# Order of VectorE's routing chain in four routed FFNs, and products of constants in TensorE's waits

## The chip, the cores and the metric

One core of a Trainium2 chip runs the whole program once per launch. The metric is the device time in microseconds of that launch. TensorE (PE) multiplies matrices, VectorE (DVE), ScalarE (ACT) and GpSimd (POOL) work on vectors, and SyncE (SP) issues transfers, as ACT and POOL can do too.

## The reference

The kernel computes four layers of a "macaron" network on x of shape (2, 512, 256) in float32, 1024 tokens in all. Each layer is half an FFN, an attention or state-space block, and half an FFN again, each on a normalised input, without learned scale, and each added to x:

```
x = x + 0.5 * ffn(layernorm(x));  x = x + attn(layernorm(x));  x = x + 0.5 * ffn(layernorm(x))
```

- Layer 0: a routed FFN with 32 experts of width 176, six chosen per token by softmax, with a capacity of slots for each expert, and a shared expert of width 352; then a retention block.
- Layer 1: a linear map with binarised weights, and sparse attention.
- Layer 2: an FFN that mixes 8 experts, and a Mamba2 block with 8 heads.
- Layer 3: a routed FFN with 8 experts of width 176, two chosen by sigmoid, and a shared expert of width 176; then a Mamba2 block with 64 heads.

So there are four routed FFNs, two in layer 0 and two in layer 3. Each is

```
scores = softmax or sigmoid of x @ router;  top k of each token
pos    = running count of an expert's tokens: the slot of each (token, expert)
y      = sum over the chosen experts of weight * (silu(x @ wg) * (x @ wu)) @ wd
out    = y + (silu(x @ sg) * (x @ su)) @ sd          # the shared expert
```

## The kernel before

x stays on chip. The 1024 tokens are NC = 8 chunks of 128, four (CB) in each of two batches or halves. A product over 256 channels is two passes (KD = 2). Every matmul in float32 shows as two records in the trace, and a weight load (PEld) goes with each.

A routed FFN runs in these steps. The line numbers are those of the profile of the kernel before.

1. For each batch: `layernorm` makes xn (VectorE, and POOL for the root, L217 and L218), TensorE transposes it (ps_tr, L177) and xT is evicted. `logits` (L317) follows: for each of the 8 chunks two matmuls with xT as the weights and the router as the moving operand, 32 columns or 8. Transposes and logits stand in a written order on TensorE and ACT (`in_order`).
2. VectorE: the scores (L730 to L735, or L748 on ACT), `topk` (L299 to L309) which ends in the mask, and then `slot_lists`. That makes sl_pre (running counts over chunks, L425) and sl_row (a number for each chosen slot, L434 and L435); TensorE makes ps_pos from sl_pre and the mask (L427, L428); VectorE makes slot numbers from it and two one-hot tables, sl_ol and sl_oh (L454 and L456 for 32 experts, L459 and L465 for 8); TensorE multiplies these (ps_sl, L473) and turns the result (ps_slt, L493). This gives sl_get and sl_put, the row numbers for the gathers and for the rows written back. In between the mask is put on the scores (L670 to L675) and the result is sent to a table in memory.
3. `shared_unit`, once for each half, on TensorE behind the logits: for each block of the shared width (three for layer 0: 128, 128, 96; two of 88 for layer 3) pg and pu (L365), silu on ACT (L368), h = s * scale * pu on VectorE (L369), and then acc (L375), one block behind; at the end x gets acc added (L393).
4. `experts_sparse`: POOL gathers the tokens of a tile (L527), `turn_x` transposes them (ps_xe, L541), ps_gu, he, ps_he, ps_ye follow (L551 to L576), and POOL scatters the rows (L581). [...]
5. A branch holds the tiles beyond the usual number; it is not taken here. The next stage loads the rows and adds them to x (L705 to L718).

Where no order is written by hand, a scheduler picks the order of each engine's instructions from its own estimate of when their inputs are ready. `issue_after` and `in_order` are the two means to say it by hand: the first keeps what is issued inside it behind one named instruction, the second chains the instructions of the named engines in the order written.

The stages that the change touches outside of the FFNs: layer 1's start (ps_add, L711, adds the FFN's rows on TensorE), and the start of the two Mamba blocks. There the input is transposed (ps_tr, L177 in layer 2, L272 by chunks in layer 3), then come pd (the step sizes, L1620), pp (the projections, L1679, each followed by a convolution on VectorE and ACT), ps_row and ps_cum (running decays, L1646 and L1664), pb and pm (L1709, L1710), and pt (transposes of the convolved input, L1761).

Of the kernel before, what the change touches and what calls it, by code (L numbers as in the profile page):

```python
# [10 lines left out]
F32 = mybir.dt.float32  # L11
AF = mybir.ActivationFunctionType
ALU = mybir.AluOpType
# [5 lines left out]
P = 128  # L19
B, S, D = 2, 512, 256  # L20
T = B * S
NC = T // P
CB = S // P
# [60 lines left out]
class Net:  # L84
# [69 lines left out]
    def rsqrt(self, out, in_, scale=1.0):  # L154

        self.nc.scalar.activation(out, in_, AF.Sqrt, bias=self.eps, scale=scale)
        self.nc.vector.reciprocal(out, out)

    def settle(self, b, n=CB, psum=None):


        parts = self.pending.get(b, [])
        while len(parts) > CB - n:
            parts.pop(0)(psum)
        if not parts:
            self.pending.pop(b, None)
# [66 lines left out]
    def layernorm_T(self, es, psum):  # L233


        xT = es.enter_context(self.tc.tile_pool(name="xT", bufs=1)).tile([P, KD, T], F32, name="xT")
        p = es.enter_context(self.tc.tile_pool(name="ln", bufs=1))

        made = {}

        def measure(b):
            made[b] = self.scales(p, b)

        def norm(b):
            made[b] = self.layernorm(p, p.tile([P, CB, D], F32, tag="xn", name="xn"), b, *made[b])

        def turn(b, k):
            self.transpose_tokens(made[b], xT, psum, b, k)

        def row(b):  # L250
            if b in self.pending:
                by_chunks(b)
                return
            measure(b)
            norm(b)
            for k in range(KD):
                turn(b, k)

        def by_chunks(b):

            xn = p.tile([P, CB, D], F32, tag="xn", name="xn")
            ps = [psum.tile([P, S], F32, tag="mm", name="ps_tr") for _ in range(KD)]
            ms = {}
            for cc in range(CB + 1):
                if cc < CB:
                    self.settle(b, cc + 1)
                    ms[cc] = self.scale(p, b * CB + cc, b * CB + cc)
                if cc > 0:
                    j = cc - 1
                    self.centre(xn[:, j, :], b * CB + j, *ms[j])  # L270
                    for k in range(KD):
                        self.nc.tensor.transpose(  # L272
                            ps[k][:, j * P : (j + 1) * P], xn[:, j, k * P : (k + 1) * P], self.ident
                        )
            for k in range(KD):
                self.evac(xT[:, k, b * S : (b + 1) * S], ps[k])

        return xT, row, measure, norm, turn
# [30 lines left out]
        nc.vector.tensor_tensor(gt, gt, eq, ALU.add)  # L309
        return gt  # L310

    def logits(self, pool, psum, xT, wT, e):
        lg = pool.tile([P, NC, e], F32, name="lg")
        ps = psum.tile([P, NC, e], F32, tag="mm", name="ps_lg")
        for c in range(NC):
            for k in range(KD):
                self.nc.tensor.matmul(  # L317
                    ps[:, c, :], xT[:, k, c * P : (c + 1) * P], wT[:, k, :], start=(k == 0), stop=(k == KD - 1)
                )
        self.nc.vector.tensor_copy(lg, ps)  # L320
        return lg

# [28 lines left out]
        at = [(i * bw, min((i + 1) * bw, f)) for i in range(n)]  # L351
        return [(gv[:, :, a:b], uv[:, :, a:b], dv[: b - a, i, :], b - a) for i, (a, b) in enumerate(at)]

    def shared_unit(self, work, psA, psM, xT, blocks, half, scale):

        nc = self.nc
        cols = slice(half * S, (half + 1) * S)
# [2 lines left out]
        def front(gv, uv, bw):  # L360
            pg = psM.tile([P, S], F32, tag="mm", name="pg")
            pu = psM.tile([P, S], F32, tag="mm", name="pu")
            for ps, wv in ((pg, gv), (pu, uv)):
                for k in range(KD):
                    nc.tensor.matmul(ps[:bw], wv[:, k, :], xT[:, k, cols], start=(k == 0), stop=(k == KD - 1))  # L365
            s = work.tile([P, S], F32, tag="s", name="s")
            h = work.tile([P, S], F32, tag="h", name="h")
            nc.scalar.activation(s[:bw], pg[:bw], AF.Silu)  # L368
            nc.vector.scalar_tensor_tensor(h[:bw], s[:bw], scale, pu[:bw], ALU.mult, ALU.mult)  # L369
            return h  # L370

        def back(h, dv, bw, first, last):
# [37 lines left out]

    def slot_lists(self, sb, tp, psM, mask, e, n, cap, r):


        nc = self.nc
# [1 line left out]
        HI = n // LO  # L418
        ET = CT // HI
        NG = e // (ET * P // CT)  # L420

        pre = tp.tile([P, NC + 1, e], F32, name="sl_pre")
        nc.vector.memset(pre[:, 0, :], 0.0)
        for c in range(NC):
            nc.vector.tensor_tensor(pre[:, c + 1, :], pre[:, c, :], mask[:, c, :], ALU.add)  # L425
        pos = psM.tile([P, NC + 1, e], F32, tag="mm", name="ps_pos")
        nc.tensor.matmul(pos, self.ones, pre, start=True, stop=False, skip_group_check=True)  # L427
        nc.tensor.matmul(pos[:, :NC, :], self.c["lt"], mask, start=False, stop=True, skip_group_check=True)  # L428

        first = tp.tile([P, NC], F32, name="sl_first")  # L430
        nc.vector.tensor_scalar(first, self.c["icol"], float(r), float(r - 1), ALU.mult, ALU.add)
        row = tp.tile([P, NC, e], F32, name="sl_row")
        for c in range(NC):
            nc.vector.tensor_tensor_scan(row[:, c, :], self.ones[:, :e], mask[:, c, :], 0.0, ALU.mult, ALU.add)  # L434
        nc.vector.tensor_tensor(row, row, first.unsqueeze(2).to_broadcast([P, NC, e]), ALU.add)  # L435
        full = sb.tile([P, 1], F32, name="sl_full")
        nc.vector.tensor_reduce(full, pos[:, NC, :], AX.X, ALU.max)
        keep = tp.tile([P, NC, e], F32, name="sl_keep")
# [67 lines left out]
    def experts_sparse(self, ew, ps, xes, table, rows, lists, w, ex, f, tiles, per, ahead=4, wp=None):  # L506
# [28 lines left out]
            return xe  # L535

        def turn_x(n, xe, nt):
            pt = ps.tile([P, KD, nt * P], F32, name="ps_xe")
            for k in range(KD):
                for i in range(nt):  # L540
                    nc.tensor.transpose(pt[:, k, i * P : (i + 1) * P], xe[:, i, k:D:KD], self.ident)  # L541
            xeT = ew.tile([P, KD, nt * P], F32, name=f"xeT{n % 2}")
            self.evac(xeT, pt)
            return xeT
# [25 lines left out]
        def down_(n, e, js, hT, wd):  # L570
            nt = len(js)
            y = ew.tile([P, nt, D], F32, name=f"ye{n % 4}")
            py = ps.tile([P, nt, D], F32, name=f"ps_ye{n % 2}")
            for i in range(nt):
                for q in range(2):
                    nc.tensor.matmul(  # L576
# [47 lines left out]
    def moe(self, pre, names, E, F, K, FS, PER, tiles, cap, r, scores, scale):  # L624
# [6 lines left out]
        with ExitStack() as es:  # L631
# [7 lines left out]
            with ExitStack() as fs:  # L639
# [6 lines left out]
                with tc.tile_pool(name="ln", bufs=1) as lp:  # L646
                    tv = table[:, :D].rearrange("(b c p) d -> b p c d", p=P, b=B)
                    rT = self.router_weights(sb, psM, router, E)
                    tail, xns = {}, []
                    with self.in_order(tail, ("PE", "Activation")):  # L650
                        for b in range(B):
                            xn = lp.tile([P, CB, D], F32, name=f"xn{b}")
                            self.layernorm(lp, xn, b, *self.scales(lp, b))
                            xns.append(xn)
                            for k in range(KD):
                                self.transpose_tokens(xn, xT, psM, b, k)
                        s = self.logits(sb, psM, xT, rT, E)
                        for b in range(B):
                            nc.scalar.dma_start(tv[b], xns[b])
                if cap < T:  # L660
# [3 lines left out]
                    for c in range(NC):  # L664
                        nc.gpsimd.dma_start(rv[c, :, :K, :], zero.unsqueeze(1).to_broadcast([P, K, D]))
                m = sb.tile([P, NC], F32, name="m")
                scores(s, m)
                mask = self.topk(sb, s, E, K)
                get, put, full = self.slot_lists(lists, sb, psL, mask, E, PER * P, cap, r)
                nc.vector.tensor_tensor(s, s, mask, ALU.mult)  # L670
                nc.vector.tensor_reduce(m, s, AX.X, ALU.add)
                nc.vector.tensor_scalar(m, m, 1e-20, None, ALU.add)
# [4 lines left out]
                blocks = self.load_shared(sg, su, sd, FS)  # L677
                with tc.issue_after(tail["PE"]):
                    for half in range(B):
                        self.shared_unit(work, psA, psM, xT, blocks, half, 0.5)  # L680
                over = lists.tile([1, 1], I32, name="over")
                nc.vector.tensor_scalar(over, full[0:1, :], float(len(tiles) * P), None, ALU.is_gt)
            ew = es.enter_context(tc.tile_pool(name="f0e", bufs=1))
# [420 lines left out]
    def l1(self):  # L1104
# [19 lines left out]
        with ExitStack() as es:  # L1124
# [173 lines left out]


            with tc.tile_pool(name="a1m", bufs=4, space=PSUM) as psM:  # L1300
                for c in range(NC + 4):
                    if c < NC:
                        front(c)
# [262 lines left out]
    def mamba(self, pre, win, wout, nh):  # L1566
# [14 lines left out]
        with ExitStack() as es:  # L1581
# [27 lines left out]
            def decay_sums(b):  # L1609
# [29 lines left out]
                nc.vector.tensor_scalar(t1, d, 1e-18, None, ALU.max)  # L1639
                nc.scalar.activation(jb[:, bs, :], t1, AF.Ln)  # L1640
                yield

                cr = wk.tile([nh, 2, S], F32, tag="cr", name="cr", bufs=1)
                ps = psM.tile([nh, S], F32, tag="mm", name="ps_row")
# [56 lines left out]
                return conv(wb[:, :, P : 2 * P], NX + 1, b, CT[:, b * S : (b + 1) * S])  # L1701

            def products(b):
                pb = psM.tile([P, CB, P], F32, tag="mm", name="pb")
                pm = psM.tile([P, CB, P], F32, tag="mm", name="pm")
                for cc in range(CB):
# [49 lines left out]
                return taps, rest  # L1756

            def prep_back(u, m):
                pt = psM.tile([P, CB, P], F32, tag="mm", name="pt")
                for cc in range(CB):  # L1760
                    nc.tensor.transpose(pt[:, cc, :], u["xc"][:, m, cc * P : (cc + 1) * P], self.ident)  # L1761
                nc.scalar.copy(u["xt"][:, :, m * P : (m + 1) * P], pt)  # L1762

                n = u["g"] * NM + m
                nc.scalar.mul(u["xc"][:, m, :], u["xc"][:, m, :], dcol[:, n : n + 1])
# [178 lines left out]
            later = {}  # L1944
            tail = {}
            with self.in_order(tail, ("PE", "Activation", "DVE")):
                row(0)
                fetch_wx(*order[0])
                d0, d1 = decay_sums(0), decay_sums(1)
# [180 lines left out]
```

## Time and profile before

| What | Value |
|---|---|
| Time, median of 3 runs | 2017.6 us (2016.25 to 2018.17) |
| The profiled execution's own time | 2018.74 us |
| Its span, first to last instruction | 2016.9 us |
| Mean granted clock of TensorE | 0.923 |
| First routed FFN, start to last ps_ye | 0 to about 244 us |
| Second routed FFN | about 440 to 672 us |
| Third and fourth | about 1156 to 1265, and 1879 to 1996 us |
| Mamba block of layer 2, of layer 3 | from 945 us, and from 1278 to 1876 us |

How to read the lines of the profile: in a timeline a row has the start, the length from the first to the last of the group, the engine, the line, the operation, out<-in, tile and moving size, and xN for the number of records. In brackets stands how long the engine had been idle before it, and what released it. "PE 1748.0 (87%)" is busy time and its share of the span. PEclk gives the granted clock of TensorE in 40 equal slices, in tenths of full speed. In a table of windows a row has the window, its length, and for each engine its busy time and number of instructions, then the granted clock, the DMA share and GB/s.

### The profile page before, as it was taken

How to read it: one execution, taken by the hardware profiler on the slowest of the kernel's cores; microseconds unless marked ns; L12 is line 12 of the kernel's file. 1: busy time of each engine (PE TensorE's matmuls, PEld its weight loads, DVE VectorE, ACT ScalarE, POOL GpSimd, SP SyncE). 2: the span in 40 equal slices, each digit the busy share in tenths (PEclk: the TensorE clock that was granted, in tenths of full speed). 3: DMA queues.
4: the chain of work that ended last, by engine and by line, in shares of the span. 5: the costliest groups of instructions: out<-in, count | busy, mean ns of one | idle time of the engine just before them, and what ended most of it. 6: DMA issues, size and time to landing. Idle time of an engine off the chain costs nothing. (4 is left out here: it accounts for less than half of the span.)

```text
span 2016.9 us, 29547 instructions
## 1 busy us (share of the span) xinstructions
PE 1748.0 (87%) x10566; PEld 1243.7 (62%) x10566; DVE 1145.4 (57%) x2673; ACT 796.8 (40%) x1340; POOL 903.6 (45%) x889
## 2 busy tenths in 40 slices
PE   6899769788999678789788989589999899999885
PEld 4677636465777545454465457357777677777564
DVE  4433276226333376556584643478777787777533
ACT  1123224311233134301661012268777677777111
POOL 3477655310777430100140026136657456767253
PEclk9899989888999889979897989699999999999788
DMA  8266440050556600000230013434454444543133
GB/s 312 82 189 190 147 178 12 11 167 13 170 185 185 214 27 1 2 21 1 95 106 22 3 54 98 137 123 149 152 168 147 147 147 159 172 149 118 44 97 96
DMA packets 117439, 226.47 MB, mean 112 GB/s; under 512 B 22382, under 2 KB 68828, under 8 KB 117014
## 3 DMA queue, kind: packets, MB, share of 16 engines
q1 hardware_dynamic: 88134, 170.17, 25.8%
q0 software_dynamic: 20608, 48.45, 7.5%
q10 hardware_dynamic: 8528, 5.72, 0.9%
q8 instruction: 92, 1.51, 0.3%
q14 instruction: 77, 0.63, 0.1%
HBM read 195.59 MB, written 41.81 MB: 118 GB/s over the span
## 5 line engine op out<-in xcount | busy, mean ns | idle before, releaser
L527 POOL DMA_INDIRECT xe<-table,sl_get x176 | 180.3, 1024 | 211.1 <-DVE sl_get L503 122.0
L551 PE MATMUL ps_gu<-we,xeT 128*128 128x352 f32 x704 | 234.2, 476 | 3.1 <-DVE xeT L130 3.1
L581 POOL DMA_INDIRECT rows<-ye,sl_put x176 | 176.8, 1005 | 82.7 <-issue 41.4
L1686 DVE SCALAR_TENSOR_TENSOR xc<-pp,L_attn_cols,xc 128x511 f32<-128x511 f32 (+2 forms) x216 | 161.4, 747 | 28.7 <-ACT xc L1682 23.4
L576 PE MATMUL ps_ye<-we,hT 88*128 88x256 f32 x704 | 168.1, 379 | 2.9 <-ACT ye L132 1.7
L556 DVE SCALAR_TENSOR_TENSOR he<-se,xe,ps_gu 128x176 f32<-128x176 f32 x176 | 69.9, 397 | 176.1 <-ACT se L555 167.0
L551 PEld LDWEIGHTS ps_gu<-we,xeT 128*128 128x128 f32 x704 | 130.8, 197 | 62.1 <-issue 6.0
L576 PEld LDWEIGHTS ps_ye<-we,hT 88*128 88x128 f32 x704 | 133.4, 190 | 36.5 <-ACT ye L132 3.6
L1813 PE MATMUL pz<-xT,wt 128*128 128x128 f32 x1152 | 143.3, 278 | 12.4 <-ACT xt L1762 6.2
L1789 DVE SCALAR_TENSOR_TENSOR lm<-lm,jb,top 128x128 f32<-128x128 f32 x576 | 153.6, 341 | 0.0
L1679 PE MATMUL pp<-xT,wx 128*128 128x512 f32 x288 | 143.2, 621 | 4.8 <-issue 1.6
L1813 PEld LDWEIGHTS pz<-xT,wt 128*128 128x128 f32 x1152 | 135.9, 193 | 17.8 <-issue 9.3
L555 ACT ACTIVATE se<-ps_gu 128x176 f32<-128x176 f32 x176 | 55.8, 317 | 228.2 <-PE ps_gu L551 228.2
L1898 PE MATMUL yacc<-wt,y 128*128 128x256 f32 x576 | 143.0, 391 | 0.9 <-POOL y L1868 0.6
L1868 POOL TENSOR_TENSOR y<-y,sg 128x512 f32<-128x512 f32 x72 | 91.8, 1274 | 106.3 <-DVE y L1867 104.8
L1806 POOL TENSOR_TENSOR ce<-ce,CT 128x1024 f32<-128x1024 f32 x54 | 127.9, 2369 | 0.0
L1898 PEld LDWEIGHTS yacc<-wt,y 128*128 128x128 f32 x576 | 104.0, 190 | 23.7 <-issue 10.1
L1518 PE MATMUL ps_y<-w8T,xT 128*128 128x512 f32 x256 | 118.4, 617 | 0.0
L1841 PE MATMUL py<-lm,xt 128*64 128x128 f32 x1152 | 108.2, 282 | 10.6 <-DVE lm L1798 3.9
L1798 DVE TENSOR_TENSOR lm<-lm,M 128x1024 f32<-128x1024 f32 x72 | 87.2, 1215 | 46.7 <-ACT lm L1794 44.1
L1879 POOL TENSOR_TENSOR sqs<-sqs,sq 128x512 f32<-128x512 f32 x56 | 71.3, 1274 | 89.0 <-ACT sq L1878 89.0
L217 POOL TENSOR_SCALAR ln_rstd<-ln_mv 128x4 f32<-128x4 f32 x15 | 3.5, 235 | 234.9 <-DVE ln_mv L209 223.7
(402 smaller groups left out, 3465.3 us busy)
## 6 DMA issues: line engine op xcount, KB each, us to landing
lm<-rows SPq DMA_DIRECT2D x72, 512.0 KB
ce<-rows SPq DMA_DIRECT2D x54, 512.0 KB
rows<-zero POOLq DMA_DIRECT2D x16, 768.0 KB, 9.4
y<-rows SPq DMA_DIRECT2D x16, 768.0 KB
we<-in_L_ffn_w_gate_dram SPq DMA_DIRECT2D x64, 176.0 KB
we<-in_L_ffn_w_up_dram SPq DMA_DIRECT2D x64, 176.0 KB
we<-in_L_ffn_w_down_dram SPq DMA_DIRECT2D x64, 176.0 KB
we<-in_L_ffn_w_dram SPq DMA_DIRECT2D x48, 176.0 KB
```

Source lines behind the costliest of these rows:

```text
L527: nc.gpsimd.indirect_dma_start(xe[:, i, :], None, table, bass.IndirectOffsetOnAxis(get[:, e * per + j : e * per + j + 1], 0), bounds_check ...
L551: nc.tensor.matmul(pg, xeT[:, k, i * P : (i + 1) * P], wgu[:, :, k], start=(k == 0), stop=(k == KD - 1))
L576: nc.tensor.matmul(py[:, i, :], hT[:, q, i * P : (i + 1) * P], wd[:, q, :], start=(q == 0), stop=(q == 1))
L581: put_rows = nc.gpsimd.indirect_dma_start(rows, bass.IndirectOffsetOnAxis(put[:, e * per + j : e * per + j + 1], 0), y[:, i, :], None, bou ...
L1518: nc.tensor.matmul(ps, xT[:, k, cs], self.w8T[:, k, 2 * e2 : 2 * e2 + 2, :], start=(k == 0), stop=(k == KD - 1))
L1679: nc.tensor.matmul(pp, wv[:, k, :], xT[:, k, b * S : (b + 1) * S], start=(k == 0), stop=(k == KD - 1))
L1686: nc.vector.scalar_tensor_tensor(out[:, 3 - w :], pp[:, : S - 3 + w], cw[:, m, w : w + 1], out[:, 3 - w :], ALU.mult, ALU.add)
L1789: nc.vector.scalar_tensor_tensor(k["lm"][:, h, :], k["lm"][:, h, :], jb[:, k["c"], n : n + 1], top, ALU.add, ALU.min)
L1806: nc.gpsimd.tensor_tensor(k["ce"], k["ce"], ct, ALU.mult)
L1813: nc.tensor.matmul(pz[:, m, :], u["wz"][:, kk, m * P : (m + 1) * P], xT[:, kk, c * P : (c + 1) * P], start=(kk == 0), stop=(kk == KD - 1),)
L1841: nc.tensor.matmul(py[i * HP : (i + 1) * HP, m, :], w[:, h * HP : (h + 1) * HP], v[:, h, :], start=(m == 0 and n == 0), stop=(n == len(src ...
L1898: nc.tensor.matmul(yacc[cc // 2][:, cc % 2, :], k["y"][:, m, :], u["wo"][:, m, :], start=(u["g"] == 0 and m == 0 and cc % 2 == 0), stop=(u ...
```

## The change

There are two kinds of edit.

VectorE's order. In each routed FFN the scores, the top k and the counts (sl_pre, sl_row and sl_first, now in `slot_counts`) are chained on VectorE. The multiplications h of the first half of the shared expert are kept behind the last of them; those of the second half are free as before.

Products of constants. A helper, `warm`, issues n matmuls identity times a 128x256 constant into a PSUM tile that nobody reads. They are put: four ahead of each batch's transposes in a routed FFN, one between the logits of each two chunks (7), two ahead and two behind the first `turn_x` of the experts, 18 at the start of layer 1, and in the Mamba blocks at the start (4 in layer 2, 18 in layer 3), between the chunks' transposes in layer 3 (3), ahead of ps_row (4), of pb (4), and of one pt (3). The branch that isn't taken gets some too; 141 are executed.

```diff
+    def warm(self, psum, n, tag="mm", w=256):
+        ps = psum.tile([P, S], F32, tag=tag, name="warm")
+        for _ in range(n):
+            self.nc.tensor.matmul(ps[:, :w], self.ident, self.c["le"][:, :w], start=True, stop=True)
...
                     self.centre(xn[:, j, :], b * CB + j, *ms[j])
+                    if j < CB - 1:
+                        self.warm(psum, 1)
...
-    def logits(self, pool, psum, xT, wT, e):
+    def logits(self, pool, psum, xT, wT, e, warm=False):
...
+            if warm and c < NC - 1:
+                self.warm(psum, 1)
...
-            nc.vector.scalar_tensor_tensor(h[:bw], s[:bw], scale, pu[:bw], ALU.mult, ALU.mult)
+            with self.tc.issue_after(behind) if behind else nullcontext():
+                nc.vector.scalar_tensor_tensor(h[:bw], s[:bw], scale, pu[:bw], ALU.mult, ALU.mult)
...
+    def slot_counts(self, tp, mask, e, r):
+        nc = self.nc
+        first = tp.tile([P, NC], F32, name="sl_first")
+        nc.vector.tensor_scalar(first, self.c["icol"], float(r), float(r - 1), ALU.mult, ALU.add)
+        pre = tp.tile([P, NC + 1, e], F32, name="sl_pre")
+        nc.vector.memset(pre[:, 0, :], 0.0)
+        for c in range(NC):
+            nc.vector.tensor_tensor(pre[:, c + 1, :], pre[:, c, :], mask[:, c, :], ALU.add)
+        row = tp.tile([P, NC, e], F32, name="sl_row")
+        for c in range(NC):
+            nc.vector.tensor_tensor_scan(row[:, c, :], self.ones[:, :e], mask[:, c, :], 0.0, ALU.mult, ALU.add)
+        nc.vector.tensor_tensor(row, row, first.unsqueeze(2).to_broadcast([P, NC, e]), ALU.add)
+        return pre, row
...
         def turn_x(n, xe, nt):
+            if n == 0:
+                self.warm(ps, 2, tag="ps_ye1")
...
+            if n == 0:
+                self.warm(ps, 2, tag="ps_ye1")
...
                         for b in range(B):
+                            self.warm(psM, 4)
                             xn = lp.tile([P, CB, D], F32, name=f"xn{b}")
...
-                        s = self.logits(sb, psM, xT, rT, E)
+                        s = self.logits(sb, psM, xT, rT, E, warm=True)
...
-                scores(s, m)
-                mask = self.topk(sb, s, E, K)
-                get, put, full = self.slot_lists(lists, sb, psL, mask, E, PER * P, cap, r)
+                with self.in_order(tail, ("DVE",)):
+                    scores(s, m)
+                    mask = self.topk(sb, s, E, K)
+                    counts = self.slot_counts(sb, mask, E, r)
+                get, put, full = self.slot_lists(lists, sb, psL, mask, *counts, E, PER * P, cap, r)
...
-                        self.shared_unit(work, psA, psM, xT, blocks, half, 0.5)
+                        self.shared_unit(work, psA, psM, xT, blocks, half, 0.5, None if half else tail["DVE"])
...
             with tc.tile_pool(name="a1m", bufs=4, space=PSUM) as psM:
+                self.warm(psM, 18)
...
+                if b == 0:
+                    self.warm(psM, 4)
                 cr = wk.tile([nh, 2, S], F32, tag="cr", name="cr", bufs=1)
...
             def products(b):
+                if b == 0:
+                    self.warm(psM, 4)
...
             def prep_back(u, m):
+                if u["b"] == u["g"] == 0 and m == 2:
+                    self.warm(psM, 3)
...
             with self.in_order(tail, ("PE", "Activation", "DVE")):
+                self.warm(psM, 4 if few else 18)
```

In the instruction streams the counts of POOL, SP, ACT and VectorE are the same before and after, and TensorE has the products of constants in addition. What moves besides: on TensorE the first acc goes behind the pg and pu of all three blocks and behind ps_pos in layer 0, and in layer 3 ps_pos goes ahead of the acc of the first half; on VectorE the three or two h of the first half go behind sl_row, the steps on the scores (L670 to L675) go ahead of the sl_row scans, the first half's two additions of acc go behind sl_oh (in layer 3 behind its first step), and sl_get goes one place ahead in the last three FFNs. On ACT the transfer of the scores' table goes one place ahead in the two FFNs of layer 0.

## The prediction

> **What bounds the kernel now.** I read section 1 and the slices of the page first, then the timelines of TensorE and VectorE in the four routed FFNs and at the starts of the attention stages, then windows of the granted clock.
>
> ```profile
> PE 1748.0 (87%) x10566; PEld 1243.7 (62%) x10566; DVE 1145.4 (57%) x2673; ACT 796.8 (40%) x1340; POOL 903.6 (45%) x889
> PEclk9899989888999889979897989699999999999788
> ```
>
> TensorE is busy 87% of 2016.9 us, at a granted clock of 0.923 on average. The windows show 1.00 or 0.50, so (1 - 0.923) x 2 x 2016.9 = 310 us ran at half clock. The slices below 9 are the seams between stages. In the expert loops TensorE is busy 20.00 of 20.00 us at clock 1.00, so what a seam saves is carried to the end. The second routed FFN (from 440 us) shows such a seam; first TensorE, then VectorE:
>
> ```profile
> 449.92 6.88 PE L317 MATMUL ps_lg<-routerT,xT 128*128 128x32 f32 x32
> 456.61 3.76 PE L365 MATMUL pg<-xT,wsh 128*128 128x512 f32 x4
> 460.16 2.96 PE L365 MATMUL pu<-xT,wsh 128*128 128x512 f32 x4
> 462.95 1.88 PE L365 MATMUL pg<-xT,wsh 128*128 128x512 f32 x4
> ...
> 472.84 0.65 PE L427 MATMUL ps_pos<-sl_pre,cst 128*128 128x288 f32 x2
> ...
> 507.81 5.06 PE L551 MATMUL ps_gu<-we,xeT 128*128 128x352 f32 x8 [0.78 <-DVE xeT L130]
> ```
> ```profile
> 463.23 0.69 DVE L369 SCALAR_TENSOR_TENSOR h<-s,pu 128x512 f32<-128x512 f32 x1 [2.58 <-PE pu L365]
> 466.66 0.69 DVE L369 SCALAR_TENSOR_TENSOR h<-s,pu 128x512 f32<-128x512 f32 x1 [0.73 <-PE pu L365]
> ...
> 475.26 0.69 DVE L393 TENSOR_TENSOR x<-x,acc 128x512 f32<-128x512 f32 x1
> ...
> 477.32 6.56 DVE L454 TENSOR_SCALAR sl_ol<-sl_hl 128x256 f32<-128x256 f32 x32
> 483.79 7.09 DVE L456 SCALAR_TENSOR_TENSOR sl_oh<-sl_hl,sl_row 128x256 f32<-128x256 f32 x16
> ```
>
> The same four matmuls of pg take 3.76 us cold and 1.88 warm; the first ps_gu takes 5.06 against 2.53 later. ps_sl (490.93) waits for sl_oh, so VectorE's chain from the logits to sl_oh sets when the gathers and the experts start. Inside it stand h, which wait for a pu that the cold clock delays, and two adds of acc that nothing urgent needs. The fourth FFN shows the same (h waits 2.47 and 2.61 us), the third less (1.27 and 2.62). In the first FFN VectorE is busy without a break from 34.64 to 61.9.
>
> How the clock moves is seen at the third FFN (columns: window, length, busy time of PE, PEld, DVE, ACT and POOL, clock, DMA):
>
> ```profile
> 1158.63:1162.05 3.42, 3.42 (x19) 3.42 (x17) 1.38 (x2) 1.17 (x2) 1.75 (x4) 0.50 0.02 5
> 1162.05:1165.46 3.41, 3.41 (x29) 3.20 (x30) 0.23 (x1) 0.00 (x0) 0.00 (x0) 1.00 0.90 306
> 1165.46:1168.88 3.42, 3.42 (x5) 1.08 (x4) 1.74 (x20) 3.31 (x4) 0.00 (x0) 0.50 0.01 4
> ```
>
> It changes at steps of 3.41 us. A stretch of transposes brought it up; the next, full of logits matmuls (8 columns on a 128x128 weight load), brought it down again though PE is marked busy throughout. So logits alone do not hold it, and long products do.
>
> **The change, part by part.** A warm product is 128x256 in float32, two records as ps_ye has them (its 4 records advance by 0.86 us): 0.43 us at full clock, 0.86 at half. 141 are executed, 76 in the FFNs (19 in each) and 65 in three attention stages: 61 us at full clock. What counts is how much of that stands in front of work that was ready.
>
> First FFN. VectorE is gated by ACT's exponential at 34.19, so warm products before the logits cost nothing and bring nothing; the cover is that wait (6.03 us), and without it they would cost 3 us. The two adds of acc (1.37 us) leave the chain, waits for ps_pos come back: -0.5. In front of the experts the clock is low from 76.61 to 83.44; two warm products before ps_xe (hidden in the wait for xe) and two behind it (0.86 us against the 0.78 that xeT takes) should keep it up: ps_gu 5.06 -> about 3: -2.0.
>
> Second FFN. Four warm products before each batch's transposes lie in waits of 2.29 and 2.44 us (1.72 needed). Second transposes 2.30 -> about 1.0. Logits: 32 records near 0.093 us (the warm rate that the third FFN shows) are 3.0 us, with 7 warm products 6.0 instead of 6.88. Their end moves from 456.83 to 455.2. At 1.72 us for each of pg and pu the third pu ends at 465.5; VectorE without its waits (2.58, 0.73, 0.35) has its counts by about 465, so ps_pos, now behind the third pu, runs at 465.6 to 466.7. Then 2.1 us of the old steps and three h (2.0 us), which are now here: sl_ol at 471.0 instead of 477.32, -6.3. TensorE's next duty is acc (24 records, 5.2 us) and the second half (six by 1.72): done near 483.5, before sl_oh at 484.7. That cover is only about 1 us: if it fails, TensorE is the next bound and the gain shrinks by that much. First ps_gu: -2.1. Sum -8.4.
>
> Third FFN. Both xn were ready and TensorE worked without a break, so eight warm products and the seven in the logits are delay: logits end 1165.1 -> 1171.1, +6.0. Against it pg and pu are warm (3.30 and 2.26 -> 1.72 each) and the waits of 1.27 and 2.62 go; ps_pos, behind four of them, moves from 1176.67 to 1178.0; with the adds of acc out and an h in, sl_ol is 0.6 later. sl_get goes ahead of the adds (POOL was released at 1194.71 by the add, 0.8 after sl_get): -0.5. ps_gu, after an idle of 5.06 us that four products do not fill, may still start cold: -0.8, between 0 and -2.5. Sum -0.7.
>
> Fourth FFN. Here both batches of transposes wait (2.02 and 2.43), logits end 1896.33 -> 1894.5, ps_pos 1907.67 -> 1901.5, two adds out, one h in: sl_ol 1910.81 -> 1904.0, -6.8; ps_gu -0.8. Sum -7.6.
>
> Attention starts:
>
> ```profile
> 686.16 5.22 PE L711 MATMUL ps_add<-y,cst 128*128 128x256 f32 x12 [12.91 <-DMA y<-rows]
> 1278.08 0.66 PE L272 MATMUL ps_tr<-cst,xn 128*128 128x128 f32 x2 [13.24 <-DVE xn L198]
> 1283.90 3.68 PE L1620 MATMUL pd<-wb,xT 128*128 128x64 f32 x16 [0.57 <-DVE xT L130]
> 1287.37 5.84 PE L1679 MATMUL pp<-xT,wb 128*128 128x512 f32 x8
> ```
>
> L3's Mamba: the other engines resume at 1268.59, so 18 warm products run from there, first at half clock, and end near 1277.7, inside the wait for xn; three more lie between the chunks. pd 3.68 -> 1.9 and pp 5.84 -> 3.44 would be -4.2; the later warm groups stand in waits of 2.72 and 2.51 us and save pp at 1301.84 (3.74) 1.9 more, but VectorE is busy 8.87 of 10 us there and keeps most of it. I take -4.5, between -8 and +1. L1's start: the same 18 from about 680.1 end near 689.8, so the first ps_add, released at 686.16, starts 3.6 us late but runs 2.6 instead of 5.22: +1; the DMA share there is 0.96 to 1.03 and y comes no earlier, so 0, between -2 and +4. L2's Mamba: four warm products stand before transposes that waited only 1.19 us: +1.7; the cold pp (3.78, 2.69, 3.38 instead of 1.88) give about -3: -1.5, between -4 and +3.
>
> SP, POOL and ACT issue the same instructions in the same order (ACT's table DMA moves one place ahead, between two silu with idle time around); no queue is moved past another.
>
> [...]
>
> Sum: -2.5 - 8.4 - 0.7 - 7.6 - 4.5 + 0 - 1.5 = -25.2. The profiled execution took 2018.74 (span 2016.9 and 1.84 around it), 1.1 above the median of 2017.6: 1993.5 from the one, 1992.4 from the other; I say 1993.
>
> **Rivals.** (1) The order pays, the warm products only pay for themselves: ps_pos then comes behind cold pg and pu (end of the third pu 469.8, sl_ol -2.0; L3's two -3.6 each; -0.5): with sl_get -10 to -11, 2007. For it: four logits stretches of 3 us added work, and window phases that differ between executions. Against it: the halved durations. (2) The warm products hold the clock nearly everywhere, TensorE's second half in the FFNs included, and Mamba's conv chains follow: -38, 1980. (3) Slower: warm products stand in TensorE's queue ahead of ready work and the clock does not rise[...]. Then a logits stretch costs 6.88 + 7 x 0.86 = 12.9 us, the third FFN +15, the groups of 18 take 15.5 us each and end at 695.6 and 1284.1, behind work that was ready at 686.16 and 1278.08 (+9 and +6, with 2.6 more between L3's chunks), L2 +3.4: +36 in all, while the second and fourth FFN lose their gain: 2053 at full price. It decides from about half of the places on (half of +36, half of -25: +5, 2023). For it: a window full of logits records did bring the clock down. Against it: 256 columns are eight times the logits' 32, and ps_ye of that size runs at 1.00. (4) Nothing to tell: the order's gain meets the delays within 0.2% (4 us, which is about what a measurement of this kernel can tell from no change).
>
> **Numbers.** Forecast 0.53 (1986 to 2001), rival 1 0.23, rival 2 0.12, rival 3 0.08, rival 4 0.04. The range 1978 to 2011 takes in the first two and most of the third. Faster 0.88, same 0.04, slower 0.08.
>
> **Signs.** In the profile after: no wait of h for pu ahead of sl_pre; ps_pos near 465.6 and 1901.5 (each stage's own shift allowed); sl_ol about 6 us earlier in FFNs two and four, unchanged in three; logits with warm products near 6.0 us; pd near 1.9 in L3; mean clock near 0.95 or above. I am wrong if the clock stays near 0.923 (then rival 1 or 3), or if ps_sl waits for the second half's pu instead of sl_oh.

## The result, and the profile after

The changed kernel took 2001.72 us (median of four, 1999.13 to 2004.27) against 2017.64: a ratio of 0.9922, 95% interval 0.9905 to 0.9939. It is 15.9 us faster, where 24.6 were forecast. A second set of runs gave the same ratio, 0.9922 (0.9903 to 0.9940).

The page of the profiled execution (1999.13 us, so the quickest of the four) has busy time by engine and the granted clock in 40 slices:

```profile
PE 1774.9 (89%) x10848; PEld 1271.5 (64%) x10848; DVE 1148.2 (57%) x2673; ACT 797.3 (40%) x1340; POOL 904.5 (45%) x889
PEclk8999979899999988979897999899999999999998
```

The mean clock is 0.950 instead of 0.923, so (1 - 0.950) x 2 x 1997.3 = 200 us ran at half clock instead of some 310. In both profiles the granted clock is recorded as 1.00 or 0.50 and nothing else; it changes 67 times before and 55 times after, and within 0.01 us all changes of a profile lie on one grid of 3.41 us. (Ahead of the first change, at 62.96 and 18.82 us, 1.00 is recorded, but in the kernel before the first pg, at 27.05, took 3.76 us, and after it the first products, at 12.10, took 3.61 where the same eight records took 1.89 later: these stretches are missing from the half-clock time.) TensorE has 282 records and 282 weight loads more, two of each for each of the 141 products, and is busy 27 us longer, in a span 20 us shorter. The second FFN's seam, in the timelines of TensorE and of VectorE:

```profile
459.19 1.96 PE L376 MATMUL pg<-xT,wsh 128*128 128x512 f32 x4
460.99 1.88 PE L376 MATMUL pu<-xT,wsh 128*128 128x512 f32 x4
...
469.58 0.66 PE L450 MATMUL ps_pos<-sl_pre,cst 128*128 128x288 f32 x2
...
504.33 2.63 PE L571 MATMUL ps_gu<-we,xeT 128*128 128x352 f32 x8 [0.19 <-DVE xeT L130]
```
```profile
471.19 0.68 DVE L381 SCALAR_TENSOR_TENSOR h<-s,pu 128x512 f32<-128x512 f32 x1
...
472.12 0.67 DVE L381 SCALAR_TENSOR_TENSOR h<-s,pu 128x512 f32<-128x512 f32 x1
...
474.62 6.55 DVE L470 TENSOR_SCALAR sl_ol<-sl_hl 128x256 f32<-128x256 f32 x32
```

pg runs warm (at full clock: 1.00 is granted from 448.90 on) from its first record, 1.96 against 3.76 us; the h wait for nothing; and the first ps_gu takes 2.63 instead of 5.06. Since the stage began 3.6 us later than before (at the end of the retention block's last product), sl_ol at 474.62 instead of 477.32 is 6.3 us earlier by the stage's own time. The reason for the late start stands in the first FFN, on VectorE; the kernel before comes first, then the changed one:

```profile
43.85 0.29 DVE L1102 TENSOR_SCALAR row_L_ffn_bias<-row_L_ffn_bias 128x256 f32<-128x256 f32 x1
...
48.42 6.55 DVE L454 TENSOR_SCALAR sl_ol<-sl_hl 128x256 f32<-128x256 f32 x32
```
```profile
43.69 0.29 DVE L1126 TENSOR_SCALAR row_L_ffn_bias<-row_L_ffn_bias 128x256 f32<-128x256 f32 x1 [5.37 <-DMA row_L_ffn_bias<-in_L_ffn_bias_dram]
...
53.24 0.68 DVE L381 SCALAR_TENSOR_TENSOR h<-s,pu 96x512 f32<-96x512 f32 x1 [2.07 <-PE acc L387]
...
54.83 6.56 DVE L470 TENSOR_SCALAR sl_ol<-sl_hl 128x256 f32<-128x256 f32 x32
```

An instruction of layer 1, which scales a bias row, has been put into the middle of the first FFN's routing chain and waits there for its own load; sl_ol is at 54.83 instead of 48.42. In the kernel before it stood behind the sl_pre steps, at 43.85, and waited for nothing.

Stage by stage in the profiled executions (the last column is the changed kernel's repetition, 1997.92 us in all; negative is a gain over before). A routed FFN ends with its last ps_ye, a Mamba block with its last yacc; the second FFN begins at the end of the retention block's last product, and layer 1's row ends with the last product of layer 2's first FFN (ps_y), so that the products ahead of the Mamba block count to that block:

| Stage | forecast | changed | again |
|---|---|---|---|
| first FFN | -2.5 | +3.6 | +0.8 |
| second FFN | -8.4 | -9.9 | -9.4 |
| layer 1, with layer 2's first FFN | 0 | -0.3 | +0.4 |
| layer 2's Mamba block | -1.5 | -0.4 | -0.3 |
| third FFN, with layer 2's second FFN | -0.7 | -0.5 | -1.1 |
| layer 3's Mamba block | -4.5 | -2.5 | -2.8 |
| fourth FFN | -7.6 | -10.0 | -10.0 |

### The profile page after: what moved, and what is told of

Read it like the earlier page. It is cut to its first block, busy times and chain, and to the rows that moved or that the text cites. A ratio compares the mean times of both kernels' runs of the same rounds, so it can differ in the third digit from the quotient of the medians.

```text
span 1997.3 us, 30116 instructions
## 1 busy us (share of the span) xinstructions
PE 1774.9 (89%) x10848; PEld 1271.5 (64%) x10848; DVE 1148.2 (57%) x2673; ACT 797.3 (40%) x1340; POOL 904.5 (45%) x889
## 5 line engine op out<-in xcount | busy, mean ns | idle before, releaser
L571 PE MATMUL ps_gu<-we,xeT 128*128 128x352 f32 x704 | 224.6, 460 | 0.2 <-DVE xeT L130 0.2
L571 PEld LDWEIGHTS ps_gu<-we,xeT 128*128 128x128 f32 x704 | 126.3, 190 | 55.7 <-DVE xeT L130 1.6
```

The source lines that it names most:

```text
L571: nc.tensor.matmul(pg, xeT[:, k, i * P : (i + 1) * P], wgu[:, :, k], start=(k == 0), stop=(k == KD - 1))
```

## The experiments

The runs fell on different chips: the kernel before took 2020.0 us on the one, 2105.5 and 2104.1 on two others. So a time is read against the kernel before on the same chip, as a ratio.

**The bias row held back.**

```diff
                 nc.vector.tensor_scalar(self.bwT[:, k, :], ps, 0.5, None, ALU.mult)
-            nc.vector.tensor_scalar(self.hb, self.hb, 0.5, None, ALU.mult)
+                last = nc.cur_bb.bb.instructions[-1]
+            with tc.issue_after(last):
+                nc.vector.tensor_scalar(self.hb, self.hb, 0.5, None, ALU.mult)
```

> The changed kernel, but the scaling of layer 1's bias row is held behind layer 1's weight preparation, so that it no longer stands in VectorE's first routing chain. Theory: in the profile of the changed kernel that one instruction waited 5.37 us for its DMA with the whole chain behind it, and what followed (ps_pos at half clock, an h that waits 2.07 us for acc) came from it; so 6 to 8 us less than the changed kernel, 1994 to 1996 us, and sl_ol of the first FFN at 47 to 49 us instead of 54.8. Rival: the first FFN is bound by the transfers of the start (the gathers or the expert weights come no earlier), then under 2 us are won, about 2001 us.

Measured: 2092.55 us against 2105.5, 0.9936 (0.9911 to 0.9961). In the profile the wait is gone and sl_ol of the first FFN is at 50.26 (47 to 49 was expected), but h of the third block still waits 1.40 us for acc, directly ahead of sl_ol. The absolute times can't be set beside those on the first chip; the changed kernel itself was run again:

> The changed kernel itself, beside the runs of before on the same chip. If the bias row's wait is a real cost and not an accident of one execution, the ratio to before lies above that of the late-bias run on a chip where both were run (0.9936), by about 0.3% (5.4 us and what follows). If it is accidental or hidden, the ratio is the same.

Measured: 2003.77 us against 2020.04, 0.9922. The same bias instruction in this execution:

```profile
41.37 0.30 DVE L1126 TENSOR_SCALAR row_L_ffn_bias<-row_L_ffn_bias 128x256 f32<-128x256 f32 x1 [1.31 <-DMA row_L_ffn_bias<-in_L_ffn_bias_dram]
...
50.98 0.69 DVE L381 SCALAR_TENSOR_TENSOR h<-s,pu 96x512 f32<-96x512 f32 x1 [2.13 <-PE acc L387]
```

It waited only 1.31 us here, since the row landed 2 us earlier and the chain arrived 2 us later. The late-bias kernel a second time:

> The late-bias kernel a second time, now wanted on the chip on which the changed kernel gave 0.9922. The second profile of the changed kernel showed a wait of only 1.31 us for the bias row where the first had 5.37, so the price hangs on when the transfer lands: 1.5 to 6 us faster than the changed kernel's 2003.8 us by this, ratio 0.989 to 0.991. If the gain is eaten by h's wait for acc (1.4 to 2.1 us), the ratio is 0.992 again.

Measured: 2088.09 us against 2104.05, 0.9913 (0.9883 to 0.9944). The two ratios of the late-bias kernel, 0.9936 and 0.9913, lie on both sides of the changed kernel's 0.9922. So what the removal of the wait is worth cannot be told in the total: it is smaller than the scatter of these runs. In the chain itself it can. From VectorE's first step behind the exponential to sl_ol the first FFN takes 13.78 us before, 21.24 and 17.23 in the two profiles of the changed kernel, and 14.89 and 14.90 in those with the late bias. The bias row cost 6.3 and 2.3 us there; the 1.1 us that stay are about the new wait of h for acc (1.40 and 1.32 us).

**The two halves of the change, each alone** (both with the late bias).

```diff
     def warm(self, psum, n, tag="mm", w=256):
+        return
```

> As the run with the late bias, but no product of constants is issued anywhere: VectorE's order alone. The prediction's first rival said -10 against the kernel before, 2007 us, because ps_pos now stands behind a pg and pu that still run at half clock. If the order needs the products (the clock) to pay, it comes out at 2012 or above. If the products are only ballast, it comes out at the late-bias run's time, 1995 us, or below.

```diff
-                with self.in_order(tail, ("DVE",)):
-                    scores(s, m)
...
+                scores(s, m)
...
-                        self.shared_unit(work, psA, psM, xT, blocks, half, 0.5, None if half else tail["DVE"])
+                        self.shared_unit(work, psA, psM, xT, blocks, half, 0.5, None)
```

> As the run with the late bias, but VectorE's chain and the hold on h are undone (h goes where the scheduler puts it, as before); all products of constants stay. By the prediction's working the products are worth about 15 of 25 us: 2003 us. If the two parts were separate, this and the order alone would add up to the late-bias run; if VectorE's waits for pu are the real cost, the warm pu comes earlier, the waits shrink by themselves, and the two together bring less than the sum.

> The products alone a second time, beside the late-bias run. The stretches from the end of the logits to sl_ol say what VectorE's order is worth with the products there: FFN one -1.6 (it costs), two +1.1, three and four -0.6 and -0.2, together a cost of about 1 us; so within 2 us of the late-bias run. By the prediction's share for the order (-10) it would be 10 us slower than the late-bias run.

Measured, as ratio to before:

| | first chip with 2105 | second with 2104 |
|---|---|---|
| order alone | 0.9981 (0.9964 to 0.9997) | |
| products alone | 0.9925 (0.9906 to 0.9944) | 0.9925 (0.9893 to 0.9957) |
| both, late bias | 0.9936 (0.9911 to 0.9961) | 0.9913 (0.9883 to 0.9944) |

The products alone give 16 to 17 us (their intervals reach from 9 to 22), which is all that both together give. The order alone gives 4 (0.6 to 7.6). The profiles say it more sharply. The time from the end of the logits to the start of sl_ol agrees within 0.1 us between the executions of one kernel in the second to fourth FFN (the kernel before and the order alone have one profile each):

| us | FFN 2 | FFN 3 | FFN 4 |
|---|---|---|---|
| before | 20.52 | 14.62 | 14.48 |
| order alone | 18.01 | 13.51 | 13.18 |
| products alone | 16.34 | 9.30 | 9.06 |
| both | 15.26 | 9.86 | 9.24 |

With the products in place the order is worth 1.1 us in the second FFN and costs 0.6 and 0.2 in the others. Why, is seen at h in the second FFN with the products alone:

```profile
489.80 0.69 DVE L381 SCALAR_TENSOR_TENSOR h<-s,pu 128x512 f32<-128x512 f32 x1
...
493.08 0.69 DVE L381 SCALAR_TENSOR_TENSOR h<-s,pu 128x512 f32<-128x512 f32 x1 [0.58 <-PE pu L376]
...
498.24 0.68 DVE L381 SCALAR_TENSOR_TENSOR h<-s,pu 96x512 f32<-96x512 f32 x1
```

h stands inside the top k as before, but the warm pu is there in time: waits of 2.58, 0.73 and 0.35 us have become 0, 0.58 and 0. With the order alone it is the other way round, on TensorE:

```profile
492.00 3.76 PE L377 MATMUL pg<-xT,wsh 128*128 128x512 f32 x4
...
498.33 1.88 PE L377 MATMUL pg<-xT,wsh 128*128 128x512 f32 x4
...
501.77 1.88 PE L377 MATMUL pg<-xT,wsh 128*96 128x512 f32 x4
...
505.20 0.65 PE L451 MATMUL ps_pos<-sl_pre,cst 128*128 128x288 f32 x2
```

VectorE's h wait for nothing, but ps_pos (for which VectorE waits 2.64 us) stands behind a pg and pu that still run cold (3.76 us for the first pg, where a later one takes 1.88).

**No products between the logits** (this run and the next start from the products alone, with the late bias).

```diff
-                        s = self.logits(sb, psM, xT, rT, E, warm=True)
+                        s = self.logits(sb, psM, xT, rT, E)
```

> As the run of the products alone, without the seven products between the logits' chunks in each routed FFN. Theory: these hold the clock so that pg and pu run warm, which is what shortens VectorE's waits; without them the stretch from the end of the logits to sl_ol is 14.5 us in layer 3's FFNs again (9.1 to 9.3 with them), and the run is 8 to 12 us slower than with them. Rival: the products ahead of the transposes already hold the clock; then each FFN wins the 3 us that the seven cost, and it is up to 10 us faster.

Measured: 2014.93 us against 2020.04, 0.9968 (0.9956 to 0.9980). Set against 0.9925 for the products alone (other chips), some 9 us are lost. TensorE in the fourth FFN, and below it VectorE:

```profile
1889.24 1.89 PE L164 MATMUL warm<-cst 128*128 128x256 f32 x8
1890.97 1.28 PE L184 MATMUL ps_tr<-cst,xn 128*128 128x128 f32 x8
1892.09 3.64 PE L326 MATMUL ps_lg<-routerT,xT 128*128 128x8 f32 x32
1895.58 3.35 PE L376 MATMUL pg<-xT,wsh 128*88 128x512 f32 x4
```
```profile
1901.04 0.68 DVE L381 SCALAR_TENSOR_TENSOR h<-s,pu 88x512 f32<-88x512 f32 x1 [2.48 <-PE pu L376]
...
1904.47 0.68 DVE L381 SCALAR_TENSOR_TENSOR h<-s,pu 88x512 f32<-88x512 f32 x1 [2.61 <-PE pu L376]
```

The logits take 3.64 us, and from 1891.90 to 1895.30 the granted clock is 1.00. pg comes directly behind them, without a gap, and takes 3.35 where the next one takes 1.88 (in the kernel before it took 3.49 there). The stretch to sl_ol is 14.62 us again (before 14.48 to 14.62). So the seven products do not pay by faster logits (with them the logits of the second FFN take 6.7 us in the changed kernel); they pay by what stands behind.

**No products around the first turn of the experts.**

```diff
-            if n == 0:
-                self.warm(ps, 2, tag="ps_ye1")
```

(twice, ahead of the turn and behind it)

> As the run of the products alone, without the two and two around the first turn of the experts. The prediction gave them 2.0 + 2.1 + 0.8 + 0.8: 5.7 us slower. If POOL's gathers set the pace of the first tiles, no difference.

Measured: 2012.12 us against 2020.04, 0.9958 (0.9942 to 0.9974), some 7 us above the products alone by ratio. The first ps_gu of the second and of the fourth FFN, then the same in the changed kernel's fourth:

```profile
502.56 4.44 PE L567 MATMUL ps_gu<-we,xeT 128*128 128x352 f32 x8 [0.78 <-DVE xeT L130]
...
1920.27 5.06 PE L567 MATMUL ps_gu<-we,xeT 128*128 128x352 f32 x8 [0.78 <-DVE xeT L130]
```
```profile
1911.22 1.10 PE L164 MATMUL warm<-cst 128*128 128x256 f32 x4 [0.87 <-DVE x L405]
...
1914.40 2.63 PE L571 MATMUL ps_gu<-we,xeT 128*128 128x352 f32 x8
```

**No products in the attention stages** (from both parts with the late bias).

```diff
-                self.warm(psM, 18)
...
-                self.warm(psM, 4 if few else 18)
```

(and the 25 others in the Mamba blocks and between the chunks of layer 3's)

> As the run with the late bias, but without the 65 products of constants at layer 1's start and in the two Mamba blocks; those of the FFNs stay. The prediction gave them -6 (L3 -4.5, L2 -1.5, L1 0): then 6 us slower than the late-bias run, about 2001 us. The profile of the changed kernel reads -2.4, -2.2 and +1.5: then 3 us slower, 1998 us. If they cost more than they bring, it is as fast or faster.

Measured: 2096.29 us against 2105.5, 0.9949 (0.9932 to 0.9966); 3.7 us above the late-bias run on the same chip, inside the intervals of both. By the stages of the table: layer 2's Mamba block 125.8 us instead of 123.5, layer 3's 615.6 instead of 611.8, layer 1's row 273.8 instead of 273.3. A single profile doesn't price the products, though. The order alone has none in layer 2's block either, and there it takes 123.7 us, 2.1 less. The two run the same instructions from ps_y to the first pp, at the same distances; first the windows and pp of the order alone, then those without attention products:

```profile
1006.27:1009.68 3.41, 3.40 (x20) 2.61 (x21) 0.94 (x5) 0.67 (x3) 0.00 (x0) 1.00 0.01 2
1009.68:1013.10 3.42, 3.42 (x10) 1.45 (x8) 3.21 (x11) 1.82 (x3) 1.26 (x2) 1.00 0.00 0
...
1008.23 3.68 PE L1709 MATMUL pp<-xT,wb 128*128 128x512 f32 x8
```
```profile
1007.83:1011.24 3.41, 3.06 (x20) 2.35 (x19) 0.97 (x4) 0.87 (x3) 0.00 (x0) 1.00 0.01 2
1011.24:1014.65 3.41, 3.41 (x5) 1.33 (x4) 2.85 (x10) 0.74 (x2) 0.84 (x2) 0.50 0.00 0
...
1010.34 5.38 PE L1703 MATMUL pp<-xT,wb 128*128 128x512 f32 x8
```

(The windows of the order alone are counted back, in steps of 3.41 us, from the next change of its clock, at 1016.51.) The window that holds pd (8 columns) ends 1.45 us into pp in the one and 0.90 us in the other; behind it 1.00 is granted in the one and 0.50 in the other, where pp takes 1.70 us more. So the same instructions at the same distances, with the grid of 3.41 us at another place against them, made 2.1 us of difference in this stage between two executions.

**Less where work was ready** (trimmed: from the products alone, with the late bias).

```diff
                         for b in range(B):
-                            self.warm(psM, 4)
+                            if self.calls != 3:
+                                self.warm(psM, 4)
...
-                self.warm(psM, 18)
...
-                self.warm(psM, 4 if few else 18)
+                if not few:
+                    self.warm(psM, 18)
```

> As the run of the products alone, without those that stood in front of ready work in the profile of the changed kernel: the eight ahead of the third FFN's transposes, layer 1's 18 and the four at the start of layer 2's Mamba. If they are ballast, 3.8 + 1.5 + 1.7 us go and it is 5 to 7 us faster than the products alone. If they pay for themselves by the clock behind them, it is the same or slower.

> The products alone, less the eight ahead of the third FFN's transposes (the trimmed run without these, layer 1's 18 and layer 2's four gave 0.9891). In the trimmed run's profile the third FFN was 3.5 us shorter than in the changed kernel's, and layer 1 and layer 2's Mamba together longer by about 6: so 3 us faster than the products alone and up to 6 faster than the trimmed run, 1994 to 1998 us, ratio 0.987 to 0.989. If layer 1's difference is only the phase of the clock's windows, it equals the trimmed run, 0.989.

> VectorE's order and the products with the late bias, less the eight products ahead of the third FFN's transposes. A second look at the order: if it is worth nothing beside the products, this is within 2 us of the products less the third; by the prediction's share it would be 10 us faster.

Measured: trimmed 1999.53 us against 2020.04, 0.9891 (0.9872 to 0.9910). The products less the third FFN's eight 2082.05 against 2104.05, 0.9892 (0.9865 to 0.9918). Both parts less these eight 2086.97, 0.9898 (0.9863 to 0.9933): 4.9 us more than the products less the eight, where at most 2 were expected, but inside the intervals. The eight cost 3 us: from the last yacc of layer 2's Mamba block to the end of the third FFN's logits it is 104.0 and 103.6 us in the two profiles of the products alone and 100.5 in that of the same less the eight; with both parts 103.5 (late bias, twice) and 100.5. The windows of the trimmed run show why nothing is lost without them:

```profile
1152.59:1156.01 3.42, 2.69 (x15) 2.50 (x16) 2.11 (x8) 0.00 (x0) 1.77 (x5) 0.50 0.02 7
1156.01:1159.42 3.41, 3.41 (x17) 3.39 (x16) 1.27 (x2) 1.17 (x2) 1.49 (x4) 0.50 0.00 0
1159.42:1162.83 3.41, 3.41 (x25) 3.19 (x24) 0.00 (x0) 0.00 (x0) 0.00 (x0) 1.00 0.91 308
1162.83:1166.25 3.42, 3.42 (x21) 2.73 (x22) 0.22 (x1) 0.46 (x1) 0.00 (x0) 1.00 0.02 5
```

The window up to 1159.42 holds transposes (until 1158.2), the first logits and only the first product's begin, and behind it 1.00 is granted. The next holds logits and products in turn, and behind it 1.00 is granted again; in the kernel before, where that window held logits and the first 0.4 us of pg, it was 0.50. Layer 2's four products neither cost nor pay. With them its Mamba block takes 123.2 to 123.5 us in ten profiles, without them (trimmed) 123.3: they start its transposes 1.80 us later (2.99 us behind ps_y instead of 1.19), and what follows is as much shorter. Layer 1's 18 show nothing that stands out of the spread of that stage (271.4 to 278.0 us with them, 271.7 to 278.0 without).

The trimmed kernel and the products less the third's eight are the best of the set, by 0.3% over the changed kernel's ratio. The intervals touch, so that they beat it is likely rather than certain.

## Why the prediction was right, and where it was not

Right in the direction and in the main mechanism: with the products the mean clock is 0.950 instead of 0.923 (on one chip 0.934 to 0.939 in the runs of the products alone, 0.907 to 0.924 in those of the order alone, 0.904 to 0.921 in those of the kernel before), pg and ps_gu behind them run warm (1.96 and 2.63 us in the second FFN), VectorE's waits for pu go, and both FFNs with waits ahead of their transposes gain most. The signs came as named: on each stage's own time ps_pos starts at 466.0 and 1902.0 (465.6 and 1901.5 forecast), sl_ol is 6.3 us earlier in the second and in the fourth FFN, pd takes 2.00, and ps_sl waits for sl_oh. Only sl_ol of the third FFN did not stay where it was (below), and the logits with products take 6.7 us, where 6.0 was booked.

The total alone doesn't decide it. 2001.7 lies between the forecast, 1993, and rival 1, 2007, just above the forecast's own band (1986 to 2001). The halves run alone decide: rival 1 had the order pay and the products pay only for themselves, and it is the other way round. Rival 2, a clock held nearly everywhere, would have given 1980, and rival 3, a clock that doesn't rise, a slower kernel; the clock of 0.950 and the gain speak against both. The sum also holds misses that cancel in part: the first FFN is 6.1 us worse than forecast, layer 3's Mamba block 2.0 and layer 2's 1.1, the fourth FFN 2.4 and the second 1.5 better.

**The bias row (first FFN, -0.5 at sl_ol; measured +6.4, and +4.1 in the repetition).** The prediction counted what the diff moves and took VectorE's chain in the first FFN as unchanged but for two adds. That step failed: chaining the steps made the scheduler put layer 1's bias row ahead of the mask's last two steps, and its load lands late in the start's transfers (11.9 us after its issue before, 14.8 after). The new h of the third block in front of sl_ol, which waits 1.4 to 2.1 us for acc, was not foreseen either. These two waits, 5.37 + 2.07, are more than the 6.1 us between forecast and profile in this stage.

**The order's share (-10).** This estimate failed. It held that the order gains 10 us even without the products, since it takes the waits of h for pu out of VectorE's chain. Alone it gave 4 us. Beside the products it gave nothing that the runs can tell, since with the products alone these waits are already down to 0, 0.58 and 0 us (second FFN). So where the forecast for sl_ol was good (-6.3 for the second FFN), it was good as a sum, with a part of it credited to the wrong edit. The single terms: second FFN -2.0, measured -2.5 for the order alone; layer 3's two -3.6 each, measured -1.1 and -1.3. In the fourth FFN of the order alone, the scheduler also put the third pg and half of a pu ahead of ps_pos, so that it ended 11.3 us behind the logits instead of 11.9: hardly any gain from a freed VectorE, because TensorE had become the one that is late. The products' share, 15 in the forecast, came out at 16 to 17, which the runs can't tell apart.

**The experts' start (-2.0, -2.1, -0.8, -0.8).** Measured from sl_ol to the last ps_ye: -2.8, -3.6, -2.7 and -3.7. In layer 3's FFNs TensorE sat idle for 5 us there, which four products were said not to fill; the kernel before, fourth FFN:

```profile
1930.21 1.14 PE L541 MATMUL ps_xe<-cst,xe 128*128 128x128 f32 x4 [5.12 <-DMA xe<-table,sl_get]
```

acc filled it: 16 of its records lie behind ps_sl now instead of 8 (with the products alone too), so only 0.87 us of idle was left in front of the products. Without the four, waits of 1.01, 1.33 and 0.78 us stand ahead of ps_gu, and it was cold (5.06 us).

**The third FFN (-0.7).** The number held, -0.5 and -1.1, in part by luck. The cost was where the prediction put it: the logits end 6.9 and 6.3 us later against the stage's start (+6.0 forecast). But sl_ol is 2.1 and 1.5 us later instead of 0.6, and the experts' start won 2.7 instead of 1.3. Taking the eight away won about 3 us.

**The attention stages (-6).** 3.7 us measured by leaving all out, inside the intervals. L2's four products at the start were booked as +1.7 and delay its transposes by 1.8; but what follows won only as much, not the -3 booked, and the first pp takes 3.68 us as before. In L3, pp was booked at 3.44 and took 5.35: pd was warm (2.00), but behind the window from 1274.91 to 1278.33, in which TensorE was busy 2.45 us, most of it with pd's 64 columns, the granted clock was 0.50 until 1281.74:

```profile
1276.31 2.00 PE L1645 MATMUL pd<-wb,xT 128*128 128x64 f32 x16 [0.67 <-DVE xT L130]
1278.15 5.35 PE L1706 MATMUL pp<-xT,wb 128*128 128x512 f32 x8
```

**The rest.** The profiled executions sum to -19.6 and -20.9 in span; the medians moved by 15.9 and 16.3. The kernel with products took 1999.13 to 2004.27 in four runs and 1997.92 to 2010.65 in six, the one before 2016.25 to 2018.17 in four and 2016.54 to 2026.84 in 27, and both profiles of the changed kernel are its quickest runs. So the table above is some 4 us better than the medians. Only one execution of each set is profiled, but every run has its mean clock: 0.951 in the quickest of the repetition and 0.944 in the longest, some 29 us more at half clock. That the grid of 3.41 us falls differently against the work from run to run, as in layer 2's block above, may be the reason; for these runs it is not shown.

What the granted clock follows is read from a few windows only. Two windows at 0.50 with 1.00 behind them, the trimmed run's up to 1159.42 and that of the kernel before up to 1162.05, were both filled mostly by transposes, with the first logits behind them; a window of the kernel before filled nearly by logits alone (up to 1165.46) had 0.50 behind it. What transposes alone do to the clock is not shown. The products alone gave 16 to 17 us, 0.8% of the time, though 61 us of them are executed by the forecast's estimate. In the profiles half-clock time fell by 109 us (from 309 to 200) for a gain of 16 in the medians. TensorE was busy in 202 of the 309 us, so most of that time was not idle; that much of it lay where nothing on the path waited for TensorE is argued, not measured.

## What to carry to other kernels

Price a clock by what waits for the cold instructions, not by the time at half clock; a few products of 256 columns between the logits (8 and 32 columns, behind which pg took 3.30 to 3.76 us in the kernel before) were worth about 9 us here although each stands in the way. When an edit shortens a wait and another removes the reason for the wait, do not add them: run each alone. Draw the border of a stage ahead of what the edit puts in front of it: four products that delay a stage by 1.8 us look like a gain of 1.8 if the count starts behind them. And in the order of a scheduler's instructions look for strangers, an instruction of another stage that waits for a transfer in the middle of a chain.

## What was not expected of the hardware

The chips differ by some 4.2% for the same kernel (2020.0 us against 2104.1 and 2105.5), and the difference lies in the expert loops: from sl_ol to the last ps_ye the four FFNs take 636.7 us in the products less the third's eight on a chip with 2104 and 546.2 in the trimmed kernel on the one with 2020, of spans of 2081.4 and 1997.7. Two stretches of the first FFN's experts (columns as above), in the same order:

```profile
100.00:150.00 50.00, 43.80 (x198) 33.29 (x197) 14.60 (x30) 11.89 (x29) 33.71 (x34) 0.97 0.52 161
```
```profile
100.00:150.00 50.00, 50.00 (x242) 39.52 (x241) 18.30 (x35) 15.11 (x35) 38.41 (x39) 1.00 0.63 191
```

TensorE is busy 43.8 of 50 us on the one and without a break on the other, at 161 and 191 GB/s. Where it stops, the profile names no releaser ("issue", 2.44 us ahead of a ps_ye), so what arrives late there is not shown. Gains ahead of the experts are kept there too: the ratio is 0.9892 for the products less the third's eight, and 0.9891 for the trimmed run on the other chip.
